# Keys and values of six groups by three float32r products in place of seven float32 block products

## The chip, the core and the metric

The kernel runs on one core of one Trainium2 chip. The metric is the time of one execution in device microseconds; the median of several runs is given, and one execution was profiled.

## What is computed

The input x has 16 sequences of 128 rows with 1024 features; a second input, the context, has the same shape. Everything is float32, cut to what matters:

```
n = layernorm(x)
Q = n @ Wq + bq                      # 1024 -> 1024, 32 heads of 32
K = ctx @ Wk + bk;  V = ctx @ Wv + bv    # 1024 -> 256, 8 heads of 32
w = softmax(Q K^T / sqrt(32))        # four query heads share a key head
x = x + (w V) @ Wo + bo
x = x + scale * (ei(layernorm(x)) @ kernel)   # kernel holds 0 and 1
```

## The kernel before

**Groups and stages.** Two sequences make a group; there are eight groups, numbered 0 to 7, and T = 256 columns hold both sequences of a group. The loop `for grp in range(NGRP)` runs the attention of group grp. Between its matmuls it does, for other groups, in this order: the output projection of the group before (`out_proj`, tiles o_u, o_c, o_v), keys and values of the next (`prep_kv`, k_u, k_c, k_v), queries of the next (`prep_q`, q_u, q_c, q_v), and the feed-forward product of the group before (`ffn`, f_u, f_c, f_v). One pass of the loop is called a stage here. Stage 1 runs from about 115 to 207 us, and later ones take some 92 us each.

**Blocks.** These products are done by Strassen's scheme in the variant with seven products and fifteen sums (`seven` and `PRODUCTS`): the operands are cut in 2 x 2 blocks, sums of the blocks of the weights are made once and kept in DRAM, sums of the blocks of the activations are made for each group. Groups 0 and 1 have plain keys and values (`prep_k`, `prep_v`). The feed-forward product alone uses float32r, a float32 whose low bits are rounded away, which TensorE multiplies in one step where it needs two instructions of two passes each for a float32: `split_now` cuts each activation in a high part hi and a low part lo, both exact in float32r, and the weights are small integers.

**Weights.** The weights of K and V stay in SBUF (`wk_sb`, `wv_sb`), and three of their block sums come from DRAM (`kv_weight_sums` makes them, by 8 operations of VectorE). All weights that are not resident come in pieces of 512 KB (`want`, `fetch`): a ring of eight buffers, filled in the order in which they are asked for. `fetch` issues the next piece when a product has finished with one, so pieces lead by eight.

**Order.** The whole order is written out at build time by the class `Stream`, which counts estimated microseconds and puts instructions on the queues of the engines: `stream.later(us, fn)` places a step after an estimated time, and the `yield` values are the estimated durations of the matmuls between. Nothing is reordered later: every engine and the DMA queue of SyncE (SP) do their instructions in this order and wait where something is not ready. A late instruction on VectorE therefore holds all that stands behind it. Eight transfers of SP can be under way: each issue waits for the eighth before it.

**Around the change.** In the group before K and V, `out_proj` reads its PSUM banks with VectorE (L876, x<-o_u and so on), which also works for the attention: maximum (L781), reciprocal (L796) and product (L797) for each of four tiles of scores; ScalarE does the exponentials (L785), the copies of transposed weights (L804, pt<-tpp) and the reads with a bias. In stage 1 VectorE also makes 16 sums of feed-forward weights (L325, wf_sb), and near 90 us ScalarE converts those weights (L301, L303). Two PSUM banks (tag mm) serve all products in turn, two others (tag tp) the transposes. `ctx_sums` makes four differences of the context per group on GpSimd (L711). `get_ctx` loads the context of the group after next by eight transfers (L166), just before K and V; `through_dram` turns rows by a store and a load (dram_x, turn_x). The reads of K and V by the old scheme are

```
if c in written:
    nc.vector.tensor_tensor(dst, both, dst, ADD)
else:
    nc.scalar.activation(dst[:, 0], both[:, 0], AF.Identity, bias=...)
    nc.scalar.copy(dst[:, 1], both[:, 1])
```

Of the kernel before, what the change touches and what calls it, by code (L numbers as in the profile page):

```python
# [9 lines left out]
FP = mybir.dt.float32  # L10
FR = mybir.dt.float32r
U8 = mybir.dt.uint8
I8 = mybir.dt.int8
AF = mybir.ActivationFunctionType
# [4 lines left out]
P = 128  # L19
# [70 lines left out]
def once(fn, *args):  # L90
    fn(*args)
    yield 0.0
# [3 lines left out]
def kernel(  # L96
# [16 lines left out]
    nc = tc.nc  # L113
    B, S, D = x.shape
    KV = Wk.shape[1]
# [8 lines left out]
    GB = 2  # L124
    T = GB * S
    HALF = 512
    assert S == P and F == D and NG == NI and NC == NA * NG
    n_exc = round(D * FRACTION_EXC)
    w_inh = -FRACTION_EXC / (1.0 - FRACTION_EXC)
# [10 lines left out]

    wk_sb = const.tile([P, NC, KV], FP, name="wk_sb")
    wv_sb = const.tile([P, NC, KV], FP, name="wv_sb")
    wf_sb = const.tile([P, 7, NC // 2, F // 2], I8, name="wf_sb")
    bqT = const.tile([P, NA, NG], FP, name="bqT")
    bkT = const.tile([P, NA], FP, name="bkT")
# [21 lines left out]
    def load_by_quadrants(dst, w, queues, *cuts):  # L169

        src = w.rearrange("(k c f) n -> k f c n", k=NB, f=32)
        n = 0
        for lo, hi in zip((0,) + cuts, cuts + (NC,)):
            for k in range(NB):
                queues[n % len(queues)].dma_start(
                    out=dst[k * 32 : (k + 1) * 32, lo:hi], in_=src[k][:, lo:hi]
                )
                n += 1

# [46 lines left out]


    PRODUCTS = ["a11 b11", "a12 b21", "s2 t2", "s1 t1", "s3 t3", "s4 b22", "a22 t4"]
    HC = NC // 2
    PIECE = 1024  # L230
    RING = 8
    feed, pieces = [], []
# [1 line left out]
    def want(src):  # L234
        feed.append(src)
        return len(feed) - 1
# [23 lines left out]
        for k in range(2)  # L260
    }

    kv_sums = {n: dram.tile([P, PIECE], FP, name=f"kv_{n}") for n in (1, 2, 4)}

    def want_kv(n):
        return want(lambda: kv_sums[n].rearrange("p (c n) -> p c n", c=1))

    def want_sum(w, n, k):
        c = 4 if w == "q" else 2
# [216 lines left out]
    def chunk(store, grp, c):  # L486
        return store[grp, c // HC][:, c % HC]
# [12 lines left out]
    def prep_k(grp):  # L500
        kv = kv_tile(grp)
        for a in range(NA):
            mm = ps_mm.tile([P, T], FP, tag="mm", name=f"k_{grp}_{a}")
            yield from accumulate(
                mm, [(wk_sb[:, c, a * P : (a + 1) * P], chunk(cTs, grp, c)) for c in range(NC)]
            )
            nc.scalar.activation(
                kv[:, a, :, 0], mm.rearrange("p (j n) -> p j n", j=GB), AF.Identity, bias=bkT[:, a : a + 1]
            )
            yield 0.85  # L510

    def prep_v(grp, batches=range(GB)):
        for j in batches:
            b = grp * GB + j
            kv = kv_tile(grp)
            mm = ps_mm.tile([P, KV], FP, tag="mm", name=f"v_{b}")
            yield from accumulate(
                mm, [(chunk(cTs, grp, c)[:, j * S : (j + 1) * S], wv_sb[:, c]) for c in range(NC)]
            )
            nc.vector.tensor_copy(kv[:, :, j, 1], mm.rearrange("p (a n) -> p a n", a=NA))  # L520
            yield 0.85
# [139 lines left out]

        return run()

    def kv_block(w, o, r):
        return w[:, r * HC : (r + 1) * HC, o * P : (o + 1) * P]

    def kv_weight_sums():

        temps = {}

        def sum_(m, n, left, right, op):
            w = (wk_sb, wv_sb)[m]

            def of(name):
                if name[0] == "s":
                    return temps[m, int(name[1])]
                return kv_block(w, int(name[1]) - 1, int(name[2]) - 1)

            if n == 3:
                dst = kv_block(w, 1, 0)  # L680
            else:
                dst = work.tile([P, HC, P], FP, tag="wide", name=f"kvs{m}_{n}", bufs=WIDE)
                temps[m, n] = dst
            nc.vector.tensor_tensor(dst, of(left), of(right), op)
            if n != 3:
                there = kv_sums[n][:, m * HALF : (m + 1) * HALF].rearrange("p (c n) -> p c n", c=HC)
                stream.later(4.0, lambda: nc.sync.dma_start(out=there, in_=dst) and None)

        us = 14.0
        for args in (  # L690
            (1, "a21", "a22", ADD),
            (2, "s1", "a11", SUB),
            (3, "a11", "a21", SUB),
            (4, "a12", "s2", SUB),
        ):
            for m in range(2):
                stream.later(us, lambda m=m, args=args: sum_(m, *args))
                us += 2.0

    ctx_parts = {}  # L700

    def ctx_sums(grp):

        half = {
            f"b{h + 1}{j + 1}": cTs[grp, h][:, :, j * S : (j + 1) * S] for h in range(2) for j in range(GB)
        }
        ctx_parts[grp] = half

        def sum_(n, left, right):
            t = half["b12"] if n == 4 else work.tile(S4, FP, tag="comb", name=f"u{n}_{grp}", bufs=4)  # L710
            nc.gpsimd.tensor_tensor(t, half[left], half[right], SUB)  # L711
            half[f"t{n}"] = t

        for n, args in enumerate(((1, "b12", "b11"), (2, "b22", "t1"), (3, "b22", "b12"), (4, "b21", "t2"))):
            stream.later(1.6 * n, lambda args=args: sum_(*args))

    def prep_kv(grp):

        ids = {p: want_kv(int(p[1])) for p in PRODUCTS if p[:2] in ("s1", "s2", "s4")}

        def run():
            half = ctx_parts.pop(grp)
            kv = kv_tile(grp)
            written = set()
            blocks = {"a11": (0, 0), "a12": (0, 1), "a22": (1, 1), "s3": (1, 0)}

            def product_of(prod, mm, start):
                left, right = prod.split()
                act = half[right]
                if prod in ids:  # L730
                    piece = pieces[ids[prod]].rearrange("p (m c n) -> p m c n", m=2, c=HC)
                    wk, wv = piece[:, 0], piece[:, 1]
                else:
                    wk, wv = [kv_block(w, *blocks[left]) for w in (wk_sb, wv_sb)]
                yield from product(
                    mm.rearrange("p (g n) -> p g n", g=NG),
                    [
                        (0, [(wk[:, c], act[:, c]) for c in range(HC)]),
                        (1, [(act[:, c], wv[:, c]) for c in range(HC)]),
                    ],  # L740
                    start,
                )
                if prod in ids:
                    fetch()

            def read(mm, c):
                o, j = int(c[1]) - 1, int(c[2]) - 1
                dst = kv[:, o, j]
                both = mm[:, : 2 * P].rearrange("p (m n) -> p m n", m=2)
                if c in written:  # L750
                    nc.vector.tensor_tensor(dst, both, dst, ADD)
                else:
                    written.add(c)
                    nc.scalar.activation(dst[:, 0], both[:, 0], AF.Identity, bias=bkT[:, o : o + 1])
                    nc.scalar.copy(dst[:, 1], both[:, 1])

            yield from seven(f"k{grp}", product_of, read)

        return run()

# [158 lines left out]
    def split(grp, name):  # L919
        def start():  # L920
            live.add(to_split.pop(0))
            split_now(grp, name)

        stream.when(lambda: to_split[0] == (grp, name) and len(live) < 4, start)

    def split_now(grp, name):
        hi = work.tile([P, HC, S], FR, tag="x2h", name=f"x2h{grp}_{name}", bufs=4)
# [201 lines left out]
    with tc.manual_schedule():  # L1129
# [102 lines left out]
        for grp in range(NGRP):  # L1232
# [5 lines left out]
            if first:  # L1238
# [7 lines left out]
                    prep_x(nxt, 0),  # L1246
                    prep_x(nxt, 1),
                    once(convert_ffn),
                    once(kv_weight_sums),
                    between(between(qs[nxt], 16, residuals, grp), 24, prep_ctx, nxt + 1, 0.0, 4.0, 8.0, 12.0),  # L1250
                )
            elif more:
                stream.add(
                    *([once(get_x, nxt)] if grp == 1 else []),
                    once(turn_rows, nxt),
                    between(os[grp - 1], 10, ctx_sums, nxt),
                    once(get_ctx, nxt + 1),
                    between(kvp[nxt], 14, load_residual, b0, 4.0),
                    between(qs[nxt], 20, prep_ctx, nxt + 1, 0.0, 5.0, 10.0, 14.0),
                )  # L1260

                stream.add(once(get_x, nxt + 1))
                if nxt < NGRP - 1:
                    stream.add(ffn(grp - 1, residual(b1, 2.0)))
            else:
                stream.add(
                    once(load_residual, p1, 1.0, "ctx"),
                    os[grp - 1],
                    once(load_residual, b0, 4.0, "ctx"),
                    ffn(grp - 2, residual(b1, 2.5)),  # L1270
                )
# [76 lines left out]
```

## Time and profile before

| what | value |
|---|---|
| median of three runs | 769.25 us (768.13 to 770.03) |
| profiled execution | 765.46 us |
| its span, first to last instruction | 763.7 us |
| granted TensorE clock | 1.000 |
| TensorE busy | 746.6 us |
| VectorE busy | 541.5 us |
| ScalarE busy | 380.2 us |
| GpSimd busy | 303.2 us |
| DMA | 203.36 MB, mean 266 GB/s |

A row of the profile names the line of the kernel, the engine, the operation, the tile written, the tiles read, and the shape; PE is TensorE, PEld its weight loads, DVE VectorE, ACT ScalarE, POOL GpSimd, SPq the DMA queue of SyncE. The printed duration of a matmul holds its way through the array, so rows overlap, and the distance between starts is what one costs. A float32 matmul appears as two instructions.

### The profile page before, as it was taken

To read this page: it belongs to the slowest core of one execution; us is meant where nothing else is said; L and a number is where in the kernel's file an instruction comes from. 1 tells how busy PE (TensorE), PEld (TensorE's weight loads), DVE (VectorE), ACT (ScalarE), POOL (GpSimd) and SP (SyncE) were. 2 spreads that over 40 slices of the span, in tenths; PEclk is the share of its full clock that TensorE was granted. 3 is DMA by queue.
4 is the path that set the end of the run, shared out by engine and by line. 5 is a ranking of instruction groups with operands and counts; after the bars stand their busy time and mean duration, and the time that the engine had idled before them with its cause. 6 is when DMAs were issued, how large, how long until landed. Compare 5 with 4: busy or idle time off the path is not lost.

```text
span 763.7 us, 14898 instructions
## 1 busy us (share of the span) xinstructions
PE 746.6 (98%) x5232; PEld 563.4 (74%) x5232; DVE 541.5 (71%) x961; ACT 380.2 (50%) x1397; POOL 303.2 (40%) x356
## 2 busy tenths in 40 slices
PE   4999999999999999999999999999999999999997
PEld 3888884699747996489855998469984699546466
DVE  1456888977787667677676687865778766769586
ACT  0245764444735455344643447434464455568363
POOL 4069830342740146401652226322274113108582
PEclk9999999999999999999999999999999999999999
DMA  9989999989499895999779995899948988752912
GB/s 229 311 319 295 372 372 412 324 272 347 158 326 267 283 319 173 316 261 294 253 244 294 297 292 201 282 314 272 316 165 297 274 274 266 240 194 83 286 45 110
DMA packets 104314, 203.36 MB, mean 266 GB/s; under 512 B 8960, under 2 KB 58432, under 8 KB 104240
## 3 DMA queue, kind: packets, MB, share of 16 engines
q1 hardware_dynamic: 102480, 200.31, 81.8%
q10 hardware_dynamic: 1248, 1.11, 0.7%
q0 software_dynamic: 512, 0.99, 0.6%
q8 instruction: 41, 0.67, 0.4%
q14 instruction: 33, 0.27, 0.1%
HBM read 170.40 MB, written 31.98 MB: 265 GB/s over the span
## 4 chain that ended last, share of the span: by engine, by line
PE 90%; DVE 7%; DMA 2%; issue 1%; ACT 0%; SPq 0%; DVEq 0%
PE q_u L558 13%; PE o_u L862 12%; PE f_u L1017 7%; PE tpp L802 7%; PE q_v L558 7%; PE o_v L862 7%; PE k_u L558 5%; PE sc L769 4%; PE av L811 4%; PE q L418 4%; PE f_v L1017 3%; PE q_c L558 3%; PE k_v L558 3%; PE o_c L862 3%; PE f_c L1017 2%; PE k L418 2%
## 5 line engine op out<-in xcount | busy, mean ns | idle before, releaser
L785 ACT ACTIVATE p<-sc,negm 128x128 f32<-128x128 f32 x512 | 181.2, 370 | 147.3 <-DVE negm L781 73.1
L781 DVE TENSOR_REDUCE negm<-sc 128x4 f32<-128x512 f32 x128 | 86.9, 682 | 72.5 <-PE sc L769 72.5
L356 POOL CAST wide<-wf_sb 128x512 fp32r<-128x512 int8 x154 | 109.2, 749 | 64.0 <-PE f_u L1017 62.7
L804 ACT COPY pt<-tpp 128x512 f32<-128x512 f32 x128 | 75.1, 595 | 96.9 <-PE tpp L802 96.3
L797 DVE TENSOR_TENSOR p<-p,inv 128x512 f32<-128x512 f32 x128 | 103.4, 808 | 4.4
L785 ACT ACTIVATION_READ_ACCUMULATOR p<-sc,negm 128x1 f32 x512 | 106.3, 208 | 0.0
L196 POOL TENSOR_TENSOR x<-x,bo_b 128x256 f32<-128x256 f32 x64 | 50.3, 806 | 87.6 <-DMA x<-in_x_dram 74.9
L558 PE MATMUL q_u<-t,piece 128*128 128x128 f32 x672 | 81.3, 275 | 0.0
L558 PEld LDWEIGHTS q_u<-t,piece 128*128 128x128 f32 x672 | 78.1, 192 | 0.2 <-issue 0.2
L802 PE MATMUL tpp<-ident,p 128*128 128x128 f32 x512 | 75.9, 273 | 1.6 <-DVE p L797 1.6
L802 PEld LDWEIGHTS tpp<-ident,p 128*128 128x128 f32 x512 | 61.3, 141 | 20.1 <-issue 13.6
L862 PE MATMUL o_v<-piece,s 128*128 128x512 f32 x128 | 60.6, 601 | 0.2 <-DVE x L876 0.2
L862 PE MATMUL o_u<-piece,s 128*128 128x512 f32 x128 | 59.7, 597 | 0.5 <-DVE x L876 0.5
L862 PE MATMUL o_u<-piece,yT 128*128 128x512 f32 x128 | 58.6, 599 | 0.0
L819 ACT ACTIVATE yT<-av,bvT 128x512 f32<-128x512 f32 x32 | 22.0, 688 | 60.3 <-PE av L811 60.3
L769 PEld LDWEIGHTS sc<-kv,qT 32*128 32x128 f32 x1024 | 31.5, 186 | 25.7 <-issue 25.7
L374 POOL TENSOR_TENSOR rs_f<-ve_f,minus_half 128x1 f32<-128x1 f32 x16 | 9.5, 595 | 96.1 <-DVE ve_f L372 83.0
L961 POOL TENSOR_TENSOR s<-turn_f,turn_f 128x512 f32<-128x512 f32 x7 | 8.9, 1277 | 97.3 <-DVE turn_f L983 71.0
L354 ACT CAST wide<-wf_sb 128x512 fp32r<-128x512 int8 x70 | 43.2, 633 | 3.3 <-PE f_u L1017 3.0
L862 PEld LDWEIGHTS o_u<-piece,yT 128*128 128x128 f32 x128 | 23.5, 190 | 28.4 <-issue 26.7
L862 PEld LDWEIGHTS o_u<-piece,s 128*128 128x128 f32 x128 | 23.0, 190 | 27.6 <-issue 22.7
L862 PEld LDWEIGHTS o_v<-piece,s 128*128 128x128 f32 x128 | 22.4, 190 | 23.3 <-issue 18.9
(155 smaller groups left out, 1493.0 us busy)
## 6 DMA issues: line engine op xcount, KB each, us to landing
piece<-o SPq DMA_DIRECT2D x64, 512.0 KB, 4.8
piece<-q SPq DMA_DIRECT2D x56, 512.0 KB, 7.1
piece<-in_L_xattn_Wq_dram SPq DMA_DIRECT2D x50, 512.0 KB, 8.0
piece<-in_L_xattn_Wo_dram SPq DMA_DIRECT2D x48, 512.0 KB, 7.1
piece<-kv SPq DMA_DIRECT2D x18, 512.0 KB, 6.9
xn<-in_x_dram SPq DMA_DIRECT2D x16, 512.0 KB, 4.6
x<-in_x_dram SPq DMA_DIRECT2D x16, 512.0 KB, 5.1
ctx<-in_ctx_dram SPq DMA_DIRECT2D x60, 128.0 KB, 7.2
```

The source lines that it names most:

```text
L196: lambda cut=cut: nc.gpsimd.tensor_add(x_t[:, cut], x_t[:, cut], bo_b[:, cut]) and None,
L356: nc.gpsimd.tensor_copy(t, wf_sb[:, FFN[name], c])
L418: nc.tensor.matmul(mm, lhsT=lhsT, rhs=rhs, start=k == 0, stop=k == n - 1)
L558: nc.tensor.matmul(mm if part is None else mm[:, part], lhsT=lhsT, rhs=rhs, start=start and n == k == 0, stop=k == len(some) - 1, skip_gro ...
L769: nc.tensor.matmul(tiles[i][:, g], lhsT=qT[rows, g], rhs=kT[rows], start=True, stop=True,)
L781: nc.vector.tensor_reduce(negm, tile_, AX.X, ALU.max, negate=True)
L785: nc.scalar.activation(p[:, g], tile_[:, g], AF.Exp, bias=negm[:, g : g + 1], accum_out=total[:, g : g + 1],)
L797: nc.vector.tensor_mul(p, p, inv.unsqueeze(2).to_broadcast([P, NG, S]))
L802: nc.tensor.transpose(tp[:, g], p[:, g], ident)
L804: nc.scalar.copy(pt, tp)
L862: nc.tensor.matmul(mm, lhsT=lhsT[:, 2 * k + c], rhs=w[:, c], start=start and k == c == 0, stop=k == c == 1, skip_group_check=True,)
L1017: nc.tensor.matmul(mm, lhsT=part[:, c], rhs=w, start=start and c == n == 0, stop=c == HC - 1 and n == 1, skip_group_check=True,)
```

## The change

Keys and values of groups 2 to 7 no longer go through `seven`. A weight w is cut in a high part H of 12 bits and L = 4096 (H - w), a value x of the context in a high part h and l = x - h. With S = H - L and s = h + 4096 l, the three float32r products H h, L l and S s give the float32 product: w x = (1 - 1/4096) (H h + L l) + S s / 4096. Each output has two halves of a PSUM bank as accumulators: the product of the high parts and that of the low parts go to the first, that of the sums to the second, and a finish adds them with factors (ScalarE, then VectorE). All matmuls have 256 columns, 24 for each of four outputs of a group.

The weights are split once, in four half tensors, by `kv_weight_parts` (ScalarE and VectorE in turn); high parts stay in SBUF in the buffers of the raw weights, low parts and sums go to DRAM and come back as eight pieces per group, where three came. The context is split for each group by `ctx_high` (ScalarE, four), `ctx_low` (GpSimd four, VectorE four). The feed-forward split of a group shares buffers with this and now also waits, when the order is written out, until the keys two groups later are done.

```
-    wk_sb = const.tile([P, NC, KV], FP, name="wk_sb")
-    wv_sb = const.tile([P, NC, KV], FP, name="wv_sb")
+    wk_sb, wv_sb = [
+        [work.tile([P, NC // 2, KV], FP, tag=w, name=f"{w}_{h}", bufs=2) for h in range(2)] for w in ("wk", "wv")
+    ]
...
-    def kv_weight_sums():
...
+    UP = 1.0 + 2.0**-13
+    DOWN = 1.0 - 2.0**-12
+    def kv_weight_parts():
+        def half_parts(w, h):
...
+            def first(q):
+                nc.scalar.activation(both[q], raw[:, 2 * q : 2 * q + 2], AF.Copy, scale=UP)
+                stream.later(1.0, lambda: second(q))
+            def second(q):
+                nc.vector.tensor_tensor(lows[q], both[q], raw[:, 2 * q : 2 * q + 2], SUB)
+                stream.later(1.0, lambda: third(q))
+            def third(q):
+                nc.scalar.activation(lows[q], lows[q], AF.Copy, scale=4096.0)
+                if q == 1:
+                    kv_high[w, h] = work.tile([P, HC, KV], FR, tag=f"w{w}", name=f"{w}h_{h}", bufs=2)
+                    for n in range(2):
+                        nc.scalar.copy(kv_high[w, h][:, 2 * n : 2 * n + 2], both[n])
+                    stream.later(2.4, lambda: [fourth(n) for n in range(2)] and None)
+            def fourth(q):
+                nc.vector.tensor_tensor(both[q], both[q], lows[q], SUB)
+                stream.later(1.5, lambda: store(q))
...
+                stream.later((6.0, 28.5, 34.5, 40.5)[n], lambda w=w, h=h: half_parts(w, h))
...
-    def ctx_sums(grp):
...
+        def high(q):
+            hi = work.tile([P, 2, T], FR, tag="x2h", name=f"ch{q}_{grp}", bufs=4)
+            nc.scalar.activation(hi, cTs[grp, q // 2][:, q % 2 * 2 : q % 2 * 2 + 2], AF.Copy, scale=UP)
...
+        def low(q):
+            lo = work.tile([P, 2, T], FR, tag="comb", name=f"cl{q}_{grp}", bufs=4)
+            nc.gpsimd.tensor_tensor(lo, cTs[grp, q // 2][:, q % 2 * 2 : q % 2 * 2 + 2], his[q], SUB)
...
+        def total(q):
+            s = work.tile([P, 2, T], FR, tag="x2l", name=f"cs{q}_{grp}", bufs=4)
+            nc.vector.scalar_tensor_tensor(s, los[q], 4096.0, his[q], MULT, ADD)
...
     def prep_kv(grp):
...
+            def finish(dst, mm, **bias):
+                nc.scalar.activation(
+                    dst, mm[:, 1], AF.Identity if bias else AF.Copy, scale=2.0**-12, **bias
+                )
+                nc.vector.scalar_tensor_tensor(dst, mm[:, 0], DOWN, dst, MULT, ADD)
...
+            for a in range(NA):
+                mm = ps_mm.tile([P, 2, T], FP, tag="mm", name=f"k_{grp}_{a}")
+                yield from pairs(mm[:, 0], "k", hi, True, ...)
+                for k, part in ((0, "l"), (1, "s")):
+                    w = pieces[ids["k", a, part]].bitcast(FR).rearrange("p (c n) -> p c n", c=NC)
+                    yield from pairs(mm[:, k], "k", (lo, s)[k], False, lambda c, act: (w[:, c], act))
                     fetch()
...
+            for j in range(GB):
...
+                    if j == GB - 1:
+                        fetch()
+                        fetch()
+                finish(kv[:, :, j, 1], mm.rearrange("p k (a n) -> p k a n", a=NA))
+            kv_done.add(grp)
...
-        stream.when(lambda: to_split[0] == (grp, name) and len(live) < 4, start)
+        stream.when(
+            lambda: to_split[0] == (grp, name)
+            and len(live) < 4
+            and (grp + 2 in kv_done or grp + 2 >= NGRP),
+            start,
+        )
...
-                    between(os[grp - 1], 10, ctx_sums, nxt),
+                    between(
+                        between(between(between(os[grp - 1], 5, ctx_high, nxt), 8, ctx_low, nxt, 0, 1), 10, ctx_low, nxt, 2),
+                        12, ctx_low, nxt, 3,
+                    ),
                     once(get_ctx, nxt + 1),
-                    between(kvp[nxt], 14, load_residual, b0, 4.0),
+                    between(kvp[nxt], 24, load_residual, b0, 4.0),
```

## The prediction

> **What bounds it now.** I read the page first, the busy times and then the chain that ended last.
>
> ```profile
> PE 746.6 (98%) x5232; PEld 563.4 (74%) x5232; DVE 541.5 (71%) x961; ACT 380.2 (50%) x1397; POOL 303.2 (40%) x356
> q1 hardware_dynamic: 102480, 200.31, 81.8%
> PE 90%; DVE 7%; DMA 2%; issue 1%; ACT 0%; SPq 0%; DVEq 0%
> ```
>
> TensorE is the bound: it is busy for 98% of the span and makes up 90% of the chain. In the view of waits it waits 3.5 us in all after its first 16 us. So a matmul saved is time saved, and any stop of TensorE is time lost. Two questions remain: what the new matmuls cost, and what the new work makes TensorE wait for. For the first I read TensorE's timeline; a cost is the distance between starts, because the printed durations overlap.
>
> ```profile
> 81.66 3.74 PE L558 MATMUL q_u<-xT,piece 128*128 128x128 f32 x32
> 85.23 3.74 PE L558 MATMUL q_c<-xT,piece 128*128 128x128 f32 x32
> 194.52 0.39 PE L1017 MATMUL f_u<-wide,x2l_s 128*128 128x512 f32 x1
> 196.11 0.39 PE L1017 MATMUL f_u<-wide,x2h_s 128*128 128x512 f32 x1
> 95.77 1.40 PE L811 MATMUL av<-pt,kv 128*32 128x512 f32 x8
> 135.00 1.92 PE L862 MATMUL o_v<-piece,s 128*128 128x512 f32 x4
> 144.21 1.05 PE L558 MATMUL k_u<-cT,wk_sb 128*128 128x128 f32 x8
> 148.26 1.13 PE L558 MATMUL k_u<-u,piece 128*128 128x128 f32 x8 [0.32 <-issue]
> 150.53 0.71 PE L558 MATMUL k_v<-u,piece 128*128 128x128 f32 x4 [0.25 <-DVE kv L751]
> ```
>
> The first pair: 32 instructions in 3.57 us, 0.1116 us each; a float32 matmul is two of them. The second pair: seven float32r steps of 512 columns in 1.59 us, 0.227 us each. The last two lines are the only waits in the keys and values of stage 1 (the pass of the loop with grp = 1): VectorE is barely in time there. So I looked at VectorE by windows and by timeline (columns of the windows: PE, PEld, DVE, ACT, POOL).
>
> ```profile
> 120.00:140.00 20.00, 20.00 (x95) 9.75 (x94) 19.73 (x36) 6.70 (x26) 7.35 (x6) 1.00 1.04 407
> 140.00:160.00 20.00, 19.43 (x144) 16.69 (x143) 19.60 (x39) 9.78 (x44) 1.93 (x3) 1.00 1.04 280
> 134.21 0.68 DVE L876 TENSOR_TENSOR x<-o_v,x 128x512 f32<-128x512 f32 x1
> 135.90 1.75 DVE L325 TENSOR_TENSOR wf_sb<-wf_sb 128x512 int8<-128x512 int8 x1
> 150.06 0.41 DVE L751 TENSOR_TENSOR kv<-k_c,kv 128x256 f32<-128x256 f32 x1
> ```
>
> VectorE is full from 120 to 160 us, in stage 1 alone; later windows hold 12 to 17 us of 20. The read of o_v ends at 134.89, and the matmuls that accumulate into that bank start at 135.00: VectorE has no slack there.
>
> **Part 1, TensorE: -11.4 us.** In stage 3 keys and values run from 327.74 to 342.12; less four transpose groups of 0.435 that is 12.6 us, for 56 float32 matmuls (112 x 0.1116 = 12.5). The new code has 2 x 3 x 8 for K and as many for V: 96 float32r matmuls of 256 columns. None is in the trace. Half of the 512-column row gives 0.1136 us; a 256-column pass of a float32 matmul is the other neighbour (L418, 64 instructions of two passes from 28.60 to 42.51: 0.1087 us a pass). I take 0.111, the middle: 10.7 us, so 1.9 us saved in each of six stages, 11.4 us (10.4 to 13.0). A switch to transposes costs nothing: between f products a transpose group and the slower matmul after it take together the same 0.44 us. The two waits of 0.6 us go, as a bank now holds 24 matmuls (2.7 us) before the next needs the other bank free, in place of 8.
>
> The Trainium skill (TensorE: Matmul & The Clock Gate, "LDWEIGHTS (loading the stationary operand)") gives a weight load as columns / 1.2 ns, 107 ns here. If these loads stood beside the matmuls, the estimate from that page would be 96 x 0.218 = 20.9 us a stage and 50 us lost in all. The trace is against this: the 0.1116 us above hold a load and a pass of 128 columns together, so the load is hidden at that rate, and the new matmuls need no faster one.
>
> **Part 2, ScalarE at 96 us: +2.9 us.** The first half of K's weights is split there: two scaled copies into sums, two of differences, two into kh, all ahead of the last pt copy in ScalarE's order.
>
> ```profile
> 94.44 1.09 ACT L301 CAST wf_sb<-raw 128x1024 int8<-128x1024 uint8 x1
> 95.49 0.59 ACT L804 COPY pt<-tpp 128x512 f32<-128x512 f32 x1
> ```
>
> ScalarE is without a gap from 91 to 96 us, and L811 at 95.77 (1.40 in place of 1.06) already waits for this copy. Six operations of 128x512 at 0.53 us from start to start (L303) are 3.2 us; nearly all of it is on the path, 2.9 us. At most 3.2, at least 0.
>
> **Part 3, VectorE in stage 1: +11.0 us.** Weight parts need 16 VectorE operations in place of 8 sums, and 12 of them now come after the scores at 114.88, where all 8 sums lay before. The price of one is 0.605 us from start to start (L684, L325). Up to the read of o_v there are 9 more, 5.4 us; 0.6 us of idle time absorbs some; and twice the operation waits for ScalarE's scaled copy, which stands behind an exponential (four of 0.34 us) or behind a store that frees its buffer: 1.2 and about 0.6 us. That read ends 6.6 us late, and TensorE stops at 135.00 for 6.6 us. Up to the next read of o_u VectorE then has xq and a wf_sb sum (2.3 us), two parts (1.2 each), two of the new combinations of the context (L756 of the new kernel, 0.75 each) and the read (0.6): 6.8 us, against 5.7 us of TensorE's own work there, so 1.1 us more. The 1.2 us are because GpSimd's four subtractions lie beside them, and the row at 135.90 shows what that does: 1.75, then 1.17 and 1.15 us for an operation of 0.68. The last combination holds k_0 by 0.9 us. K's first finish (two steps, VectorE's like L751) stands where k_c's read stood, behind three rounds of maximum, reciprocal and product: VectorE reaches its end 6.8 + 1.8 + 10.6 = 19.2 us after the late read, TensorE needs that bank for v_0 after 5.7 + 1.1 + 3.4 (the last product) + 0.9 + 5.3 (48 matmuls) + 0.4 = 16.8 us: 2.4 us more. Sum 6.6 + 1.1 + 0.9 + 2.4 = 11.0. From below 7 (no waits on ScalarE, no slowing by GpSimd), from above 13.5 (stores land 8.4 us after issue, as kv<-kvs does). Nothing returns this: TensorE is full afterwards.
>
> The Trainium skill (SBUF — State Buffer, "Who interferes with whom") has a VectorE instruction with two SBUF inputs and a GpSimd instruction that reads SBUF lock each other out whole. By that rule alone, each of the four operations could wait out a subtraction of 1.27 us, 4 x 1.87 in place of 3.9 us, and the 1.1 would be 4.7. The rows from 135.90 to 139.86 show a partial cost, and I stay with them.
>
> **Part 4, the queue of SP: +2.4 us.** Each stage now fetches 8 pieces for K and V where it fetched 3. With eight buffers, the first pieces of q can no longer be ahead of the context loads.
>
> ```profile
> 327.94 0.42 SPq L243 DMA_DIRECT2D piece<-q  x1
> 328.41 9.69 SPq L166 DMA_DIRECT2D ctx<-in_ctx_dram  x8
> 338.19 0.38 SPq L243 DMA_DIRECT2D piece<-q  x1
> ```
>
> Eight context loads hold SP for 8.0 to 9.7 us, each waiting for the eighth transfer before it. Now only the pieces of K and V precede them (kv pieces land in 6 to 7 us, the Wq ones in 8 to 9), so I put the first q piece at 7.7 us after the start of K and V. Pieces issued just after the context loads landed in 3.7 to 4.7 us: there at 12.2. TensorE asks for it at 10.7 + 1.7 = 12.4. That is even; I take 0.6 us in each of stages 2 to 5 (stage 6 has no context to load, stage 1 is late anyway), 2.4 us in all, 0 to 12.
>
> **At nothing.** GpSimd's four subtractions of the context take the place of four, at the same 1.27 us. Four combinations a stage on VectorE (2.4 us) fall in its idle times of 2.27 and 2.82 us at 316 to 322 us; without that cover they would hold the k_0 finish by 1 us a stage. ScalarE's four scaled copies fall into its half-empty output projection. The condition on split is met before it asks. The 24 stores of parts (4 MB in place of 1.5) ride in a queue whose pieces lead by eight.
>
> **The sum.** -11.4 - 0.6 + 2.9 + 11.0 + 2.4 = +4.3 us on the profiled execution's 765.46 us (span 763.7 and 1.8 around it): 769.8. The median of the runs, 769.25, is 3.8 us above that execution, so I forecast 773.5.
>
> **Rivals.** *Faster:* VectorE's lag is smaller because its operations find the gaps, or ScalarE's copies are off the path. With parts 2 to 4 together at 4 us instead of 16, it is 12 - 4 = 8 us faster: 761. For it speaks that nothing else in the trace stops TensorE; against it the 0.1 us of slack at 135.00. It decides once stage 1 costs under 7 us. *Slower, by SP:* the first q piece is late by 3.5 us in four stages, if the context loads hold SP for the 9.7 us they held it and the piece needs the 6.3 us seen at 155.6; that is 14 in place of 2.4, so 785. It decides once the piece is issued later than 8 us after K starts. *Not what it says:* float32r at 256 columns runs at half rate, +10.7 us a stage, over 830; the 0.227 us row speaks against it.
>
> **Chances.** Forecast 0.50 (own range 768 to 781), faster rival 0.28, SP 0.18, half rate 0.04. A measurement tells 0.3%, 2.3 us. Faster: 0.26 of its rival and 0.01 of the forecast's edge. Same: 0.02 and 0.11. Slower: 0.38 + 0.18 + 0.04. The range from 763 to 787 leaves out the low end of the faster rival (about 0.1) and the high ends of the others (about 0.09).
>
> **What would show it.** Right: the rows of k_ and v_ step by 0.109 to 0.114 us; the chain holds VectorE for some 10 us more, between 130 and 165 us; TensorE waits there for x<-o_v and for the kv finish. Part 2 is right if the av row near 96 us is 3 us longer. Part 4 is right if q_u waits for a DMA of Wq in stages 2 to 5 by under 1 us. Wrong: no VectorE wait over 3 us in stage 1, or waits for vs or vl pieces.

## The result, and the profile after

The changed kernel takes 807.19 us (median of four runs, 803.92 to 808.09) where the kernel before takes 768.9: ratio 1.0489, 95% interval 1.0455 to 1.0523. The direction was the likelier one of the forecast; the size was far off: 38 us more instead of 4. The profiled execution took 806.3 us, with a span of 804.5 us and a granted clock of 0.998.

The page of the changed kernel, the same three lines as before:

```profile
PE 753.4 (94%) x5136; PEld 557.1 (69%) x5136; DVE 570.6 (71%) x999; ACT 403.5 (50%) x1421; POOL 304.5 (38%) x356
q1 hardware_dynamic: 111440, 218.67, 82.6%
PE 54%; DMA 24%; DVE 14%; ACT 4%; issue 2%; SPq 1%; POOL 0%; DVEq 0%; ACTq 0%; POOLq 0%
```

TensorE is no longer full: 51 us of the span without it in place of 17. In the chain, DMA rose from 2% to 24% and VectorE from 7% to 14%. So it was not one stop in one stage. TensorE's timeline (start, duration, row, and in brackets the wait before it):

```profile
98.29 1.05 PE L892 MATMUL av<-pt,kv 128*32 128x512 f32 x2 [1.93 <-ACT pt L885]
137.60 2.46 PE L943 MATMUL o_u<-piece,s 128*128 128x512 f32 x4 [3.20 <-DVE x L957]
146.04 1.98 PE L943 MATMUL o_v<-piece,s 128*128 128x512 f32 x4 [2.18 <-DVE x L957]
167.21 0.97 PE L787 MATMUL v<-vh,ch 128*128 128x256 f32 x6 [2.65 <-DVE kv L780]
352.09 1.12 PE L787 MATMUL k<-cl,piece 128*128 128x256 f32 x8
353.05 1.12 PE L787 MATMUL k<-cs,piece 128*128 128x256 f32 x8
385.56 2.02 PE L565 MATMUL q_u<-t,piece 128*128 128x128 f32 x16 [1.48 <-DMA piece<-q]
391.02 3.36 PE L565 MATMUL q_v<-xT,piece 128*128 128x128 f32 x28 [0.78 <-DMA piece<-q]
403.60 0.50 PE L1103 MATMUL f_c<-wide,x2l_a 128*128 128x512 f32 x1 [1.05 <-DVE qT L665]
```

The first line is Part 2, the next three are Part 3, both as predicted in kind. The two k rows give the step: eight matmuls in 0.96 us, 0.120 us each, not 0.111 (the sign of being right was 0.109 to 0.114). The last three lines are from stage 3: q_u and q_v wait for pieces in the middle of the queries, not for the first piece, and the feed-forward product waits for VectorE. Neither was in the forecast.

The view by windows shows one more thing: after the wait of 3.20 us the granted clock is 0.62 from 138 to 142 us and 0.95 from 142 to 146, where the whole execution has 0.998. That is half clock for about 3.4 us, which by these numbers costs an estimated 1.7 us on top of the wait. More on this in the last section.

For all kernels below I cut the span by first rows: each column runs from the first matmul row of a product to the first of the next one, so attention and waits in between count with it. Columns: time until stage 1's output projection; that projection; keys and values of stage 1; projection with keys and values of stages 2 to 6; queries of stages 1 to 6; feed-forward product of stages 1 to 5; the rest. All in us, from one profiled execution of each kernel; that of the kernel before is 3.4 us faster than its median, and that of three_low 2.9 us, so a difference of 1 or 2 us between two rows can lie in the execution. A wait for the first piece of the queries ends a column of keys and values, and counts there.

| kernel | start | out 1 | KV 1 | out+KV 2-6 | q 1-6 | ffn 1-5 | rest | span |
|---|---|---|---|---|---|---|---|---|
| before | 116.0 | 28.2 | 15.3 | 218.2 | 190.1 | 84.6 | 111.3 | 763.7 |
| changed | 118.3 | 38.8 | 18.7 | 217.3 | 204.4 | 95.6 | 111.4 | 804.5 |
| no_fetch | 118.9 | 38.0 | 17.3 | 215.6 | 190.1 | 95.6 | 111.7 | 787.1 |
| pace | 120.3 | 37.3 | 18.6 | 216.5 | 203.0 | 84.6 | 111.8 | 792.1 |
| no_dve | 118.3 | 32.1 | 21.2 | 223.2 | 202.8 | 95.7 | 111.5 | 804.8 |
| before_dma | 116.9 | 28.2 | 17.0 | 222.5 | 202.3 | 84.5 | 111.4 | 782.9 |
| before_two | 116.9 | 28.2 | 15.3 | 219.0 | 196.1 | 84.5 | 111.4 | 771.5 |
| nf_ns | 118.6 | 37.0 | 17.6 | 215.3 | 190.1 | 95.2 | 111.4 | 785.2 |
| nf_ns_nd | 120.5 | 28.8 | 19.1 | 214.4 | 190.1 | 95.2 | 112.3 | 780.3 |
| all_out | 119.1 | 28.8 | 19.1 | 217.3 | 189.9 | 84.6 | 111.9 | 770.7 |
| three_low | 118.2 | 33.4 | 14.3 | 213.2 | 189.8 | 84.5 | 111.4 | 764.8 |
| three_low_pool | 122.7 | 30.0 | 14.4 | 214.3 | 196.4 | 84.6 | 111.4 | 773.8 |
| early | 116.3 | 27.8 | 14.5 | 214.9 | 193.1 | 84.5 | 112.3 | 763.5 |

The 40.8 us between the first two spans are 2.3 + 10.6 + 3.4 - 0.9 + 14.3 + 11.0 + 0.1. Over half of it is in the two columns that the forecast had at 2.4 and at nothing.

### The profile page after: what moved, and what is told of

Its sections match the earlier page's. It is cut to its first block, busy times and chain, and to the rows that moved or that the text cites. A ratio compares the mean times of both kernels' runs of the same rounds, so it can differ in the third digit from the quotient of the medians.

```text
span 804.5 us, 14863 instructions
## 1 busy us (share of the span) xinstructions
PE 753.4 (94%) x5136; PEld 557.1 (69%) x5136; DVE 570.6 (71%) x999; ACT 403.5 (50%) x1421; POOL 304.5 (38%) x356
## 4 chain that ended last, share of the span: by engine, by line
PE 54%; DMA 24%; DVE 14%; ACT 4%; issue 2%; SPq 1%; POOL 0%; DVEq 0%; ACTq 0%; POOLq 0%
PE o_u L943 10%; DMA piece<-q 6%; PE o_v L943 6%; DMA dram_f<-x2n 5%; PE f_u L1103 4%; PE tpp L883 4%; PE q L425 3%; DMA piece<-in_L_xattn_Wo_dram 3%; PE sc L850 3%; PE av L892 3%; PE q_u L565 3%; PE v L787 3%; PE q_v L565 3%; DVE p L878 2%; DVE negm L862 2%; PE o_c L943 2%
## 5 line engine op out<-in xcount | busy, mean ns | idle before, releaser
L363 POOL CAST wide<-wf_sb 128x512 fp32r<-128x512 int8 x154 | 112.7, 767 | 62.7 <-PE f_u L1103 54.9
L750 POOL TENSOR_TENSOR cl<-cT,ch 128x512 fp32r<-128x512 f32 x24 | 33.3, 1399 | 62.5 <-PE o_v L943 30.1
L1047 POOL TENSOR_TENSOR s<-turn_f,turn_f 128x512 f32<-128x512 f32 x7 | 8.9, 1275 | 105.3 <-DVE turn_f L1069 84.6
L943 PEld LDWEIGHTS o_v<-piece,s 128*128 128x128 f32 x128 | 22.2, 190 | 28.3 <-issue 17.9
```

Source lines behind the costliest of these rows:

```text
L363: nc.gpsimd.tensor_copy(t, wf_sb[:, FFN[name], c])
L750: nc.gpsimd.tensor_tensor(lo, cTs[grp, q // 2][:, q % 2 * 2 : q % 2 * 2 + 2], his[q], SUB)
L943: nc.tensor.matmul(mm, lhsT=lhsT[:, 2 * k + c], rhs=w[:, c], start=start and k == c == 0, stop=k == c == 1, skip_group_check=True,)
```

## The experiments

**First round: transfers, order, VectorE.** The theories: D, five more pieces per stage are more than the transfers can give in time; O, the new estimates for keys and values put the attention's instructions at other places among the queries and the feed-forward product; V, VectorE's work on the weights holds stage 1.

*no_fetch*

```
-   ids["k", a, part] = want_kv("k", a, part)      # and the four of "v"
-   w = pieces[ids["k", a, part]].bitcast(FR)...; fetch()
+   w = kv_high["k", c // HC][:, c % HC, a * P : (a + 1) * P]   # for l and s alike
```

> The changed kernel, but the eight pieces with low parts and sums are not fetched: in all six groups their matmuls read the high parts instead (so keys and values are left wrong; stores of parts stay). Order on every engine as in the changed kernel. Theory D (transfers): the five more pieces per stage are why queries take 33.1 to 35.6 us in stages 2 to 5 where they took 31.3, and by late rows of turn_f also why the feed-forward product takes 19.1 in place of 16.9. Then both go: -13 and -11, about 783 us. Theory O (order): only the queries get back, the feed-forward product stays at 19.1: about 794 us. If transfers have nothing to do with either: 806 us.

Measured: 789.44 us, ratio to before 1.0272 (1.0246 to 1.0298), 17.8 us less than the changed kernel. The queries are back at 190.1 to the tenth; the feed-forward product did not move at all. So D holds for the queries, and the feed-forward product is something else.

*pace*

```
-   yield 0.24
+   yield 0.249
```

> The changed kernel with one number changed: the estimate for two matmuls of keys and values is 0.249 us in place of 0.24, so that the sum of the estimates is that of the old scheme (11.95 us). On TensorE queries, feed-forward product and output projection then have the attention's matmuls at exactly the places of the kernel before (scores after 12 matmuls of the second-to-last q product's tile in place of 14, transposes between feed-forward products and not two matmuls into them). Theory O (order): the feed-forward product goes from 19.1 back to 16.9 in stages 1 to 5, -11 us: about 796 us, queries still 33 to 35. Theory D (transfers alone): no gain, 805 to 808 us.

Measured: 794.77 us, ratio 1.0363 (1.0308 to 1.0417), 12.4 us less than the changed kernel. The feed-forward product is back at 84.6, the queries stay at 203.0. So O holds there, and one number of the build-time clock was worth 11 us. How it acts is seen on VectorE's timeline around the start of the feed-forward product, first the kernel before, then the changed one:

```profile
368.98 0.69 DVE L781 TENSOR_REDUCE negm<-sc 128x4 f32<-128x512 f32 x1 [3.45 <-PE sc L769]
370.09 0.69 DVE L658 SCALAR_TENSOR_TENSOR qT<-q_v,qT 128x512 f32<-128x512 f32 x1 [0.42 <-PE q_v L558]
371.81 0.69 DVE L933 TENSOR_TENSOR x2l_s<-turn_f,x2h_s 128x512 fp32r<-128x512 f32 x1 [0.43 <-ACT x2h_s L930]
```

```profile
397.16 0.69 DVE L665 SCALAR_TENSOR_TENSOR qT<-q_v,qT 128x512 f32<-128x512 f32 x1 [4.10 <-PE q_v L565]
397.77 0.68 DVE L862 TENSOR_REDUCE negm<-sc 128x4 f32<-128x512 f32 x1
400.61 0.69 DVE L1019 TENSOR_TENSOR x2l_s<-turn_f,x2h_s 128x512 fp32r<-128x512 f32 x1 [1.56 <-ACT x2h_s L1016]
402.87 0.68 DVE L665 SCALAR_TENSOR_TENSOR qT<-q_u,bqs 128x512 f32<-128x512 f32 x1
```

Before, four matmuls of q_v's last product stood behind the scores, now two. Before, VectorE took the maximum (negm) while TensorE finished q_v. Now the read of q_v stands first and waits for TensorE, the maximum comes behind it, so the exponentials are later, and behind them on ScalarE the split x2h_s (399.95). VectorE waits 1.56 us for it, and behind that stands the last read of q_u, whose bank f_c needs. The view of waits has f_c for qT five times, 5.3 us, in the changed kernel and in no_fetch alike, and not in pace. The transposes now also fall two matmuls into a product of the feed-forward group, not between two.

*no_dve*

```
-   nc.vector.tensor_tensor(lows[q], both[q], raw[...], SUB)
-   nc.vector.tensor_tensor(both[q], both[q], lows[q], SUB)      # for k1, v0, v1
+   ScalarE's scaled copy reads both[q] in place of lows[q]
```

> The changed kernel, but without the twelve VectorE operations of the last three half tensors of weights (low parts and sums of them are left wrong; ScalarE's copies, stores and fetches stay). Theory V: VectorE's twelve operations are what holds the output projection of stage 1 (38.8 in place of 28.2 us) and the keys' first finish: that stage's output projection goes back to 28.2 to 30 us and keys and values to 15 to 16, -11 to -14 us: 793 to 796 us. Rival: ScalarE's scaled copies and the waits for stores set it, VectorE only stands in the waits' names: less than -4 us.

Measured: 805.24 us, ratio 1.0464 (1.0428 to 1.0501): 2 us. By the total, theory V falls; by the table it does not: the projection of stage 1 is 6.7 us shorter (38.8 to 32.1), and then keys and values are 2.6 us longer in stage 1 and, with the projections, 5.9 us in stages 2 to 6. TensorE's timeline of this kernel shows where it went:

```profile
161.07 0.98 PE L790 MATMUL v<-vh,ch 128*128 128x256 f32 x6 [3.89 <-DVE kv L783]
263.43 0.51 PE L790 MATMUL v<-piece,cs 128*128 128x256 f32 x2 [1.64 <-DMA piece<-vs]
363.08 0.50 PE L790 MATMUL v<-piece,cs 128*128 128x256 f32 x2 [2.06 <-DMA piece<-vs]
```

The first is stage 1: the wait for K's finish grew from 2.65 to 3.89 us, and a stretch of half clock follows it, so the 2.6 us there are not the transfers'. The last two are waits for pieces of V: four of them, 5.0 us, in the view of waits, and none in that of the changed kernel; the second is followed by half clock as well. A TensorE that is earlier asks earlier, and the transfers answer at their own rate.

*before_dma*

```
-   ids = {p: want_kv(...) for p in PRODUCTS if p[:2] in ("s1", "s2", "s4")}
+   order of wants: -, -, s2, s1, -, s4, -, -     # "-" is a piece that nobody reads
+   fetch() behind every product, twice behind the last
```

> The kernel before, with five more pieces of 512 KB fetched per stage into the ring and read by nobody (eight for keys and values in place of three). Theory D (transfers): queries of stages 1 to 6 get longer by about 2.4 us each, feed-forward product hardly: +12 to +15 us, about 782 us. Rival (the ring of eight covers them, and the longer time comes from the order or from VectorE): under +3 us.

Measured: 786.25 us, ratio 1.0222 (1.0178 to 1.0266): 17.9 us for five pieces a stage that nobody needs, nearly what no_fetch took away, and more than the 12 to 15 expected. Its queries are 202.3, 12.2 more than before; the view of waits names q pieces as in the changed kernel, and they land as late. Another 6.0 us are in the columns of keys and values, where the wait for the first piece of the queries counts. Bytes and places in the ring were not varied apart: no run here has pieces of another size. From its timeline and its DMA issues (count, KB, median us to landing; 7.1 before, 8.7 changed, 7.3 in no_fetch):

```profile
367.58 1.57 PE L558 MATMUL q_u<-t,piece 128*128 128x128 f32 x12 [1.33 <-DMA piece<-q]
```
```profile
piece<-q SPq DMA_DIRECT2D x56, 512.0 KB, 8.6
```

**Second round: what is left of stage 1, and another form of the three products.**

*nf_ns*: no_fetch without `stream.later(1.5, lambda: store(q))`.

> The kernel of no_fetch (789.4 us), and the 24 stores of low parts and sums are left out as well (nothing reads them there). Theory S: in stage 1 a store of a part still holds the buffer that ScalarE's next scaled copy needs (ScalarE waits 1.77 us for a store at 135.5 us in the changed kernel, VectorE 2.67 us behind it): output projection of stage 1 from 38.0 to 34 to 36 us, 785.5 to 787.5 us. Theory V: VectorE's own work is the whole limit there, the waits for stores lie in it: 789 us.

Measured: 787.94 us, ratio 1.0260 (1.0223 to 1.0298). That is 1.5 us less by medians, and the two intervals overlap; the projection is 37.0 in place of 38.0. Theory S is worth about 1 us at most.

*nf_ns_nd*: nf_ns with the edit of no_dve.

> The kernel of nf_ns, and VectorE's twelve operations for the last three half tensors of weights left out too, as in no_dve. With neither transfers nor VectorE's work, stage 1 should take what it took before: output projection 28.2 to 29 us, keys and values 14.2 to 15, so 9 to 12 us less than no_fetch: 777 to 780 us. In no_dve the same operations were worth 6.7 us there and only 2 at the end; theory D (transfers, full from stage 1 to 6, took the rest back) says that here, with the transfers gone, what stage 1 gains stays gained to the end. Rival: ScalarE's copies hold stage 1: less than 5 us gained.

Measured: 780.43 us, ratio 1.0156 (1.0126 to 1.0187): 7.5 us less than nf_ns, where the same edit was worth 2 us with the transfers in place. The projection of stage 1 is at 28.8. So VectorE's twelve operations were worth 8 us there, as theory V has it (1.7 of them by estimate for the half clock that followed the stop and is gone with it), and the transfers had taken most of the gain back. Keys and values of stage 1 did not come down to the 14 or 15 us expected, but stay at 19.1: v still waits 2.95 us for the first finish of K on VectorE (kv), followed here by half clock. That wait is a matter of the finish's place in the order and not of the weights' work; Part 3 below shows its rows.

*three_low*

```
-   both = (1 + 2**-13) w;  lows = 4096 (both - w);  both -= lows      # H, L, S
+   high = copy(w);  low = w - high                                     # H, L
-   three products into mm[:, 0], mm[:, 0], mm[:, 1]; finish: ScalarE, then VectorE
+   H h + H l + L h into one bank; finish: one operation (K ScalarE, V VectorE)
-   eight pieces per group
+   four pieces per group;  yield 0.249
```

> Three products in another form: H h + H l + L h, with L = w - H and l = x - h not scaled and no sums, so one accumulator, a finish of one operation, four pieces per stage (before 3, changed 8), 12 stores in place of 24, 8 operations of VectorE for weights in place of 16 and none for the context; pace as in the run pace. The product of the low parts is left out (about 2 to the power -24 of the result). By theory D one piece more than before costs about 17.9/5 = 3.6 us, keys and values gain 0.65 us in six stages (-4), ScalarE at 96 us +2, VectorE's eight operations, six of them in stage 1, +3 to +5: about 773 us (768 to 778). Rival: transfers decide by a threshold, not in proportion, so that one piece more costs nothing: 767 to 770.

Measured: 769.55 us, ratio 1.0025 (1.0004 to 1.0047). In the profiled execution, the fastest of ten, the rival came true: with four pieces the queries take what they took before, 189.8. The next kernels, with the same four pieces, show that this does not always hold. Projection and keys with values of stages 2 to 6 take 213.2 us, 5.0 less than before: 96 x 0.120 = 11.5 in place of 12.5 us, five times. What remains lost is in the projection of stage 1 (5.2, with a stretch of half clock in it) and ahead of it (2.2).

*three_low_pool*: the eight subtractions on GpSimd.

> The kernel of three_low with the eight subtractions of weights on GpSimd in place of VectorE. If VectorE's operations in stage 1 are what is left there: 3 to 5 us less than three_low, 768 to 770. Rival: GpSimd takes 1.27 us for each in place of 0.6 and slows VectorE beside it, and ScalarE's copies wait for it: no gain, or up to 3 us more.

Measured: 773.05 us, ratio 1.0063 (1.0033 to 1.0092); worse. The projection of stage 1 did get shorter, 30.0 in place of 33.4, but ScalarE waits 2.16 us at 98.57 for the subtraction that GpSimd queued behind its sums of Wo, the copy pt stands behind it, and av waits 3.22 us: stage 1 starts at 122.7. A wait was moved, not removed. Besides, its queries take 196.4 us, with 4.1 us of waits for q pieces, though it fetches no more than three_low.

**Third round: closing the account, and a version that puts the split where there is room.**

*all_out*: nf_ns_nd with `yield 0.249`.

> The changed kernel with all four suspects taken away at once: no fetches of parts, no stores of parts, without VectorE's twelve operations (so keys and values are left wrong), and the estimate 0.249 of the run pace. If the account is complete, it is the sum: nf_ns_nd 780.4 less 11 for five feed-forward products = 769 to 770 us; what is left over the kernel before is then ScalarE before stage 1 (+2 to +4) and keys of stage 1 (+4), less 0.65 in five stages. If a cause is missing, or pace's gain came from transfers: 773 us or more.

Measured: 771.05 us, ratio 1.0016 (0.9998 to 1.0035); 1 us above the expected range, and under the bound for a missing cause. Transfers (fetches and stores), order and VectorE's twelve operations together are 36 of the 38 us.

*before_two*: before_dma with two extra pieces in place of five.

> The kernel before, with two more pieces per stage fetched and read by nobody (five for keys and values; before 3, before_dma 8). Theory of proportion: 17.9 x 2/5 = 7 us more. Theory of a threshold (the ring and the quiet feed-forward product take up some transfers for nothing; three_low with four pieces had all its queries at 31.3 to 31.4 us): 0 to 3 us more.

Measured: 772.26 us, ratio 1.0036 (1.0011 to 1.0061): 3.1 us (0.9 to 4.7 by the interval), between the two. By the medians two extra pieces cost 1.5 us each, the next three 5 us each. Not in proportion, and not free: in the profiled execution the queries take 196.1, 6.0 more than before.

*early*

```
+   def quarter(...):                       # eight, at 13, 15, ... 25 and 28 us
+       nc.scalar.copy(high, raw)
+       nc.vector.tensor_tensor(raw, raw, high, SUB)     # 1.2 us later, then its store
+   def keep(...): kv_high <- high, from 36 us on        # ScalarE
```

> The kernel of three_low with the weights split earlier: eight quarters, each one copy on ScalarE (high part, into a buffer of its own), one subtraction on VectorE (low part, over the raw weight), then its store; they start 13 to 28 us after the point from which three_low started at 6 to 42, one at a time, so that VectorE has nearly all of them behind it when stage 1 starts, as it had the eight sums of the kernel before; the high parts go to their place by ScalarE later. three_low lost 5.2 us in the output projection of stage 1 and 2.2 us before it. If VectorE's place in stage 1 and ScalarE's at 96 us are the causes: both go, 762 to 764 us, faster than the kernel before (767.6) by 4 to 6. Rival: three_low's loss is from transfers or ScalarE's exponentials in stage 1: 768 to 770, no gain.

Measured: 765.98 us, ratio 0.9967 (0.9941 to 0.9992): faster than the kernel before by 3.2 us (0.6 to 4.5 by the interval), the only version here whose interval lies below 1. The projection of stage 1 is at 27.8, the start at 116.3: both losses of three_low are gone, as they should be if they were VectorE's place and ScalarE's at 96 us. The two were moved in one run; only the columns tell them apart. The forecast was a gain of 4 to 6 us. In the profile the queries take 3 us more than before (193.1), and TensorE waits 1.9 us for q pieces. Its page:

```profile
PE 741.7 (97%) x5136; PEld 557.6 (73%) x5136; DVE 542.9 (71%) x955; ACT 394.4 (52%) x1401; POOL 302.8 (40%) x356
PE 76%; DMA 11%; DVE 9%; issue 1%; ACT 1%; POOL 1%; SPq 1%; DVEq 0%; POOLq 0%; ACTq 0%
```

## Why the prediction was wrong

Its terms against the table's columns, in us on the span:

| column | predicted | measured |
|---|---|---|
| start (Part 2) | +2.9 | +2.3 |
| out 1 and KV 1 (Part 3, less Part 1's share) | +8.5 | +14.0 |
| out+KV 2-6 (Part 1) | -9.5 | -0.9 |
| q 1-6 (Part 4) | +2.4 | +14.3 |
| ffn 1-5 ("at nothing") | 0 | +11.0 |
| sum | +4.3 | +40.7 |

**Part 1, mis-sized by half.** The step is 0.120 us, so a stage saves 1.0 us and not 1.9. That weight loads are hidden was right: each of these matmuls has a new weight. The step could be read from the rows at hand in another way. 0.1087 us is a 256-column pass of a float32 matmul, 0.2174 for two; the float32r matmul that streams the same 512 columns takes 0.227. If the 0.010 us between them come with every instruction and do not halve with the width, the step is 0.1087 + 0.010 = 0.119, and that is what came. I took the middle of two neighbours that measured different things. The rest of the column, 4 us, went to V's wait for the two-step finish (0.24 us in each of stages 2 to 5), to late pieces (no_fetch has 1.7 less), and to stage 5, where o_v waits 1.31 us for VectorE's read at 527.31. three_low, which finishes in one step, has the full 5.0.

**Part 2, right** in place and mechanism, and a little too large: 1.93 us of wait at 98.29, stage 1 later by 2.3, where 2.9 was worked out; it is gone in early, where ScalarE gets the copies one at a time.

**Part 3, right in mechanism, too small.** The projection lost 10.6 where 7.7 was worked out (6.6 and 1.1), keys and values 3.4 where the terms give 0.8 (0.9 and 2.4, less 1.9 and 0.6). Of the 10.6, the runs put 8.2 on VectorE's twelve operations (nf_ns against nf_ns_nd) and about 1 each on stores and fetches. TensorE's waits there add up to 7.7 us; the half clock after the longest, an estimated 1.7 us, was in no term. Of the 3.4, 1.24 us are a wait for the first q piece, at 175.74. The two waits of the old scheme did go, and a longer one took their place: 2.65 us for K's first finish, which stays when the weights' work is taken away (2.95 in nf_ns_nd). VectorE does not come last there: it waits itself for ScalarE's step of the finish, which stands behind four exponentials, the last of them until 166.23.

```profile
166.21 0.48 ACT L777 ACTIVATE kv<-k,bkT 128x256 f32<-128x256 f32 x1
166.72 0.43 DVE L780 SCALAR_TENSOR_TENSOR kv<-k,kv 128x256 f32<-128x256 f32 x1 [1.19 <-ACT kv L777]
```

The prediction read the rows from 135.90 on as a partial slowing by GpSimd. They fit as well with waiting for the rest of an operation that already runs: GpSimd's subtraction of 135.50 takes 1.59 us, to 137.09, and VectorE's operation ends 0.56 us later, at 137.65. No run here decides between the two.

**Part 4, the step that failed.** I costed the eight pieces as a question of the queue: when is the first q piece issued? That term was sized well, in part by luck: the waits for the Wq pieces are 2.1 us in all, but 1.24 of them are in stage 1, which the term left out. What failed is that it saw no other wait: the queries lost 14.3 us, and no_fetch gives all of them back. I never asked whether the transfers have 2.6 MB more per stage to give. The view by windows of the kernel before warns of it (last two columns: DMA share, GB/s), for projection, keys and values, queries and feed-forward product of stage 3:

```profile
299.00:327.00 28.00, 28.00 (x119) 13.01 (x116) 21.02 (x39) 10.70 (x48) 10.16 (x10) 1.00 0.91 300
327.00:342.00 15.00, 15.00 (x130) 14.47 (x129) 12.06 (x26) 7.64 (x34) 1.10 (x2) 1.00 0.96 266
342.00:373.00 31.00, 31.00 (x319) 28.84 (x318) 19.33 (x34) 13.70 (x52) 8.41 (x9) 1.00 0.95 313
373.00:390.00 17.00, 17.00 (x114) 13.34 (x116) 13.24 (x22) 12.45 (x39) 13.82 (x20) 1.00 0.49 158
```

The transfers are busy at 0.91 to 0.96 in three windows of four, 74 us of 91, and half idle only in the feed-forward product. At 300 GB/s, 2.6 MB are 8.7 us; that a ring of eight buffers and a queue in fixed order can move only part of that into the quiet window is my reading; no run varied the ring. The share is a warning and not a limit: in no_fetch the projection and the keys and values of stage 3 (318 to 346 and 346 to 360 us) show 1.00 and 1.08, and TensorE waits for no piece; its queries (to 391.5 us) show 0.86. TensorE being the bound at 98% said nothing about how near the second bound was. The 81.8% of the queue in the page is an average over both kinds of window.

The Trainium skill (DMA: Bandwidth & Descriptors, "Where 436 GB/s comes from") holds that for transfers between HBM and SBUF the HBM side binds, at about 358 GB/s per core, half of a stack; by that figure 2.6 MB would be an estimated 7.3 us. The four rows above stay below it, at 158 to 313 GB/s, and so does the window of 347 to 381 us of before_dma with 340 GB/s. But the row of 120 to 140 us in the prediction has 407 GB/s, and the page of the kernel before a slice at 412, so 358 is no hard limit in this case.

**"At nothing", the other step that failed.** The new order cost 11.0 us in the feed-forward product, which pace gives back. I looked at the condition on split and at the work that was added, not at what the new estimates move. The sum of the estimates for keys and values fell from 11.95 to 11.52 us, and everything that the build-time clock places after them, the attention's matmuls among them, moved by up to two matmuls against the queries. That the order is written out at build time, so that the new one can be laid beside the old one before any run, was known; "a switch to transposes costs nothing" was worked out from rows in the old places.

**The rivals.** Faster needed stage 1 under 7 us. The rival by SP had late q pieces, but only the first of each stage and only by the time of its issue; most of the late ones were pieces in the middle. Half rate was wrong: 0.120 is half of 0.227 and a little more. None of them had the room of the transfers, and none had order; so the range ended at 787.

## What to carry to other kernels

Before adding a transfer, read the DMA share window by window, and only in the windows where the transfer must land, and try the extra transfers alone in the old kernel: one that TensorE bounds at 98% can be close to the next bound, and then a gain upstream can be paid back there (no_dve gained 6.7 us in one place and kept 2). Price a stop of TensorE of 2 us or more with the half clock that may follow. Where an order is written out from estimates, lay the new order beside the old one on every engine, for the untouched parts above all, and keep the sum of the estimates when a part is replaced. An estimate for a shape that no row shows should be built from a part per column and a part per instruction, and both ways of reading the difference between two rows carried through the sum.

## What the runs showed of the hardware

A float32r matmul costs 0.120 us at 256 columns and 0.227 at 512: if the rest goes with the columns, 2 x 0.120 - 0.227 = 0.013 us come with each instruction. The Trainium skill (TensorE: Matmul & The Clock Gate, "Wait — 56ns, not 53.3ns?") gives columns / 2.4 GHz + 2.5 ns on a warm array, an estimated 0.109 and 0.216 us. The float32 pass of 0.1087 us agrees with it; the float32r rows are 0.011 above it at both widths, at a granted clock of 1.00 in the windows that hold them. Why, no run here shows.

After a stop of some 2 us or more, TensorE can run at half clock for about 3.4 us. In nf_ns_nd, after the wait of 2.95 us, with the window of 162 to 164 us (clock 0.50, then DMA share and GB/s):

```profile
161.51 1.91 PE L768 MATMUL v<-vh,cl 128*128 128x256 f32 x8
163.22 1.31 PE L768 MATMUL v<-vh,cs 128*128 128x256 f32 x6
162.00:164.00 2.00, 2.00 (x11) 2.00 (x11) 2.00 (x4) 0.00 (x0) 0.00 (x0) 0.50 0.81 221
```

Eight matmuls take 1.71 us there, 0.214 each in place of 0.120. The length of the wait alone does not decide it: 1.93 us before av near 98 us are followed by half clock in pace and in nf_ns_nd, and not in the changed kernel; 2.94 us at 166.03 in nf_ns are not. Columns of single executions differ by an estimated 1.7 us for this alone.

Extra transfers do not cost in proportion to their bytes: by medians over the whole run, the first two extra pieces a stage cost 1.5 us each and the next three 5 us each, although every one of them is 512 KB. Nor is there a fixed number that comes free: with four pieces a stage the queries took 189.8, 193.1 and 196.4 us in three kernels, against 190.1 with three.
